# Softmax sums of one group of heads: from products with ones to adds on VectorE

## The chip, the cores and the metric

The kernel runs on one core of a Trainium2 chip. A core has a matrix engine (TensorE, PE in the profile, with PEld for its weight loads), VectorE (DVE), ScalarE (ACT), GpSimd (POOL) and SyncE (SP), which here only issues transfers. The metric is the device time of one execution in microseconds. The kernel before the change takes 2181.35 us (median of three runs, 2180.84 to 2181.51).

## The reference

One decoder layer on x of shape (4, 1024, 512) in float32, with a context of shape (4, 1024, 384): a gated self-attention, a cross-attention to the context, and a small feed-forward network, each behind a layer norm and each added to its input. The change lies in the cross-attention, for the last of the four batches:

```python
attn = jnp.einsum('bhqd,bhkd->bhqk', q, k) * scale      # 16 heads of 32
attn = jax.nn.softmax(attn, axis=-1)
x = jnp.einsum('bhqk,bhkd->bqhd', attn, v).reshape(B, Nq, Cq)
return x @ Wo + bo
```

The feed-forward network after it is

```python
s = jnp.einsum('btd,dm->btm', x, Win) + bin_
h = jax.nn.relu(s[..., None] * W1 + b1)                  # 16 hidden rows
g = jnp.einsum('btmh,mh->btm', h, W2) + b2
out = jnp.einsum('btm,md->btd', g, Wout) + bout
```

## The kernel before, in words

There are eight units: self-attention (phase 0) for the four batches, then cross-attention (phase 1) for the four batches. A unit is worked in two halves of 512 queries, a half in four groups of four heads (`g` is 0 to 3), a group in eight steps (`kt`), one for each block of 128 keys. A step (`step`, L725) does this:

- `scores` (L606): TensorE multiplies keys and queries for the four heads, two heads to a tile (L614). ScalarE takes the exponentials of each pair into a tile `e` of 128 x 1024 (L620). The softmax needs, for each query, the sum of the exponentials over all keys, and this sum is made in one of two ways. Either VectorE adds the tiles of the steps into an accumulator `es` (L626 in step 1, L628 after it), and at the end one product with a column of ones sums over the 128 partitions (L672). Or TensorE multiplies every exponential tile with a column of ones and accumulates the result in the PSUM tile `sm` (L650).
- `times` (L639) for the step before: TensorE multiplies values and exponentials into `av` (L642), and every second step it makes the products with ones (L650) for the second pair of heads, for two blocks of keys, four products at a time in four column groups of the array.
- then a share of other work, spread over the steps by `run` (L976): the projections, norms and network of the half before and of the next unit.

Which way is taken is set by `shared`. In phase 0, and in the last unit (`u` is 7), it is true: the first pair of heads is added on VectorE, the second pair is summed by products with ones. In the units 4 to 6 it is false and VectorE adds both pairs. The very last group of the kernel (`closing`) always adds both pairs.

One step after a group's last `times`, `normalize` (L656) copies `av` and, if `shared`, `sm` out of PSUM on ScalarE (L659, L661). One step later `add_up` (L669) makes the products with ones of the accumulators, copies them out (L673), and sends the sums to DRAM and back so that they lie spread over the partitions: with `shared` two writes (L678, L683) and two reads (L684, L688), without it one write (L678) and one read (L680). Three steps later `divide` (L693) takes the reciprocals and sends them out (L712) and back, broadcast (L716, four transfers). Three steps after that `multiply` (L721) scales `av` into `q` (L722).

Every engine and every queue works in the order in which the program issues instructions; the order is written by hand. The transfers named here are all issued by SP.

Beside group 1 of each half of the last unit lies the work of the half of the queries before: the output projection (`project`: L101 on TensorE, then the residual on VectorE, L813, and the statistics, L817 and L818), the hidden rows of the network (`hidden`: ScalarE L905, VectorE L909 and L911) and the network's outputs (`outputs`, L918: TensorE L922, VectorE L928, transfer out L930). After them come the normalized rows (`norm`, VectorE L310), their trip to DRAM and back (`away` L314, `back` L319), which with a transpose of blocks on VectorE (L325) turns them, and the first product of the network (`inputs`, L884).

The projections, the network's outputs and some of the scores use the two PSUM banks called `f`, which alternate:

```python
        def bank():
            since[0] = 0
            return pf.tile([P, HALF], F32, tag="f", name="f")
        def score_banks():
            if spare[0] and not open_[0] and since[0] >= 2:
                two = [bank(), bank()]
```

`score_banks` borrows both for one pair of heads where no other work of that step needs them; otherwise the scores use one of two tiles `s`.

Of the kernel before, what the change touches and what calls it, by code (L numbers as in the profile page):

```python
# [63 lines left out]
def moderate_path(tc: tile.TileContext, a: dict, out: bass.AP, flag: bass.AP):  # L64
    nc = tc.nc
    x = a["x"]
    with ExitStack() as st:
# [20 lines left out]
# [4 lines that stand above are left out]
                return two, [(slice(i, i + 1), b) for i, b in enumerate(two)]  # L92
            since[0] += 1
            s = ps.tile([P, 2, HALF], F32, tag="s", name="s")
            return [s[:, i, :] for i in range(2)], [(slice(0, 2), s)]
# [250 lines left out]
        order = [(ph, b) for ph in range(2) for b in range(B)]  # L346
# [5 lines left out]
        def after(steps, f, behind=False):  # L352

            soon.append((tick[0] + steps, behind, f))
# [236 lines left out]
        def attention(u, hf):  # L591

            ph, b = order[u]
# [1 line left out]
            steps = []  # L595
            sums = 2 if ph == 0 else 1

            shared = ph == 0 or u + 1 == len(order)

            def apart(g):  # L600
                return 2 if u + 1 < len(order) else 3

            def closing(g):
                return (u, hf, g) == (len(order) - 1, 1, HG - 1)

            def scores(g, kt):  # L606
                q, k = me["q", hf], me["k"]
                es = []
                for i in range(2):
                    two, reads = score_banks()  # L610
                    for j in range(2):
                        r = slice((2 * i + j) * DH, (2 * i + j + 1) * DH)
                        for m in range(0, P, 64):
                            nc.tensor.matmul(  # L614
                                two[j][m : m + 64], lhsT=k[r, g, kt * P + m : kt * P + m + 64], rhs=q[r, g, :],
                                start=True, stop=True,
                            )
                    e = p4.tile([P, 2, HALF], F32, tag="e", name="e", bufs=6)
                    for h, s in reads:
                        nc.scalar.activation(e[:, h, :] if len(reads) == 1 else e[:, h.start, :], s, AF.Exp, scale=SCALE)  # L620
                    es.append(e)
                me["e", kt] = es
                for i in range(1 if shared and not closing(g) else 2):
                    if kt == 1:
                        me.setdefault("es", {})[i] = p1.tile([P, 2, HALF], F32, tag=f"es{i}", name="es")
                        nc.vector.tensor_tensor(me["es"][i], me["e", 0][i], es[i], ALU.add)  # L626
                    elif kt > 1:
                        nc.vector.tensor_tensor(me["es"][i], me["es"][i], es[i], ALU.add)  # L628
                if ph == 0 and kt > 0:
                    if kt == 1:  # L630
                        me["eg"] = p1.tile([P, 2, HALF], F32, tag="es1", name="eg")
                    for h in range(2):
                        eg, gate = me["eg"][:, h, :], lambda t: me["sw"][:, t, HG * g + h, 1:2]
                        if kt == 1:
                            nc.scalar.activation(eg, me["e", 0][0][:, h, :], AF.Identity, scale=gate(0))  # L635
                        nc.vector.scalar_tensor_tensor(eg, es[0][:, h, :], gate(kt), eg, ALU.mult, ALU.add)  # L636
                return es

            def times(g, kt, es):  # L639
                for h in range(HG):  # L640
                    r = slice(h * DH, (h + 1) * DH)
                    nc.tensor.matmul(  # L642
                        av[r, :], lhsT=me["v"][:, kt, HG * g + h, :], rhs=es[h // 2][:, h % 2, :],
                        start=(kt == 0), stop=(kt == NT - 1),
                    )
                if shared and kt % 2 and not closing(g):

                    for j in range(4):
                        t, h = kt - 1 + j // 2, j % 2
                        nc.tensor.matmul(  # L650
                            sm[j * DH : j * DH + sums, :],
                            lhsT=me["sw"][:, t, HG * g + 2 + h, :] if ph == 0 else ones, rhs=me["e", t][1][:, h, :],
                            start=(kt == 1), stop=(kt == NT - 1),
                        )

            def normalize(g):  # L656
                i = (u * 2 + hf) * HG + g
                both = p1.tile([P, 3, HALF], F32, tag="both", name="both")
                nc.scalar.copy(both[:, 0, :], av)  # L659
                if shared:  # L660
                    nc.scalar.copy(both[:, 1, :], sm)  # L661
                    added = [me["es"][0][:, 0, :], me["es"][0][:, 1, :]]
                    if ph == 0:
                        added += [me["eg"][:, 0, :], me["eg"][:, 1, :]]
                else:
                    added = [me["es"][h // 2][:, h % 2, :] for h in range(HG)]
                after(1, lambda: add_up(g, i, both, added), behind=True)

            def add_up(g, i, both, added):  # L669

                for j, e in enumerate(added):
                    nc.tensor.matmul(sm[j * DH : j * DH + 1, :], lhsT=ones, rhs=e, start=True, stop=True)  # L672
                nc.scalar.copy(both[:, 2, :], sm)  # L673

                c, s1, s2 = cs_[i % 2], sum1_d[i % 4], sum2_d[i % 4]
                rows = both.rearrange("(j r) s q -> j r s q", r=DH)
                n = len(added)
                nc.sync.dma_start(s1[0:n], rows[0:n, 0, 2, :])  # L678
                if not shared:
                    nc.sync.dma_start(c[:, 0, 0, :], s1[0:n].rearrange("h (q e) -> (h q) e", e=INNER))  # L680
                else:
                    for k in range(sums):
                        nc.sync.dma_start(s2[k], rows[:, k, 1, :])  # L683
                    nc.sync.dma_start(  # L684
                        c[0:64, 0:sums, 0, :], s1[0:n].rearrange("(s h) (q e) -> (h q) s e", h=2, e=INNER)
                    )
                    for k in range(sums):
                        nc.sync.dma_start(  # L688
                            c[64:, k, :, :], s2[k].rearrange("(p h) (q e) -> (h q) p e", h=2, e=INNER)
                        )  # L690
                after(apart(g), lambda: divide(g, i, both, c))

            def divide(g, i, both, c):  # L693
                if shared:
                    both_ = p2.tile([P, sums, INNER], F32, tag="c2", name="both_")
                    nc.vector.tensor_tensor(both_, c[:, 0:sums, 0, :], c[:, 0:sums, 1, :], ALU.add)
                else:
                    both_ = c[:, 0:1, 0, :]
                if ph == 0:

                    den = p2.tile([P, INNER], F32, tag="den", name="den")
                    nc.vector.scalar_tensor_tensor(
                        den, both_[:, 0, :], 1e-8, me["iap", hf][:, g, :], ALU.mult, ALU.mult
                    )
                    nc.vector.tensor_tensor(den, den, both_[:, 1, :], ALU.add)
                else:
                    den = both_[:, 0, :]
                rec = p2.tile([P, INNER], F32, tag="rec", name="rec")
                nc.vector.reciprocal(rec, den)
                nc.vector.tensor_reduce(marks[:, i : i + 1], den, AX.X, ALU.add)  # L710
                nc.vector.tensor_reduce(marks[:, NS + i : NS + i + 1], rec, AX.X, ALU.add)
                nc.sync.dma_start(rec_d[i % 4].rearrange("j (q e) -> (j q) e", e=INNER), rec)  # L712

                all_ = p1.tile([P, HALF], F32, tag="recb", name="recb")
                for j in range(HG):
                    nc.sync.dma_start(  # L716
                        all_[j * DH : (j + 1) * DH, :], rec_d[i % 4][j : j + 1, :].to_broadcast([DH, HALF])
                    )
                after(apart(g), lambda: multiply(g, both, all_), behind=u + 1 < len(order))

            def multiply(g, both, all_):  # L721
                nc.vector.tensor_tensor(me["q", hf][:, g, :], both[:, 0, :], all_, ALU.mult)  # L722
                me["divided", hf] = g
# [1056 lines left out]
```

## Time and profile before

| | us |
|---|---|
| median of three runs | 2181.35 |
| the profiled execution, own time | 2181.99 |
| its span, first to last instruction | 2180.1 |
| TensorE busy | 2158.6 (99%) |
| VectorE busy | 1483.6 (68%) |
| ScalarE busy | 1278.9 (59%) |
| GpSimd busy | 121.9 (6%) |

The times in rows of the profile count from the start of the span. A row of the timeline names start, length, engine, line of the kernel, operation, output and input tiles, and in brackets the engine's idle time before it with what ended that. Rows of TensorE count records; a float32 product leaves two, so a set of four products shows as x8. The last unit's first half has its scores from about 1922 us on, its second half runs to about 2130 us. Group 1, which the change touches, has its eight steps from about 1948 to 1980 us in the first half and from about 2052 to 2084 us in the second. The clock granted to TensorE is full (1.00) in both stretches.

### The profile page before, as it was taken

To read this page: it belongs to the slowest core of one execution; us is meant where nothing else is said; L and a number is where in the kernel's file an instruction comes from. 1 tells how busy PE (TensorE), PEld (TensorE's weight loads), DVE (VectorE), ACT (ScalarE), POOL (GpSimd) and SP (SyncE) were. 2 spreads that over 40 slices of the span, in tenths; PEclk is the share of its full clock that TensorE was granted. 3 is DMA by queue.
4 is the path that set the end of the run, shared out by engine and by line. 5 is a ranking of instruction groups with operands and counts; after the bars stand their busy time and mean duration, and the time that the engine had idled before them with its cause. 6 is when DMAs were issued, how large, how long until landed. Compare 5 with 4: busy or idle time off the path is not lost.

```text
span 2180.1 us, 52850 instructions
## 1 busy us (share of the span) xinstructions
PE 2158.6 (99%) x22750; PEld 557.8 (26%) x22750; DVE 1483.6 (68%) x2158; ACT 1278.9 (59%) x1583; POOL 121.9 (6%) x175
## 2 busy tenths in 40 slices
PE   9999999999999999999999999999999999999997
PEld 4322222222222222222222222222222222222223
DVE  3477575786756866556666666877877777766567
ACT  0156545655456554566666666675757667577774
POOL 2000010040210101000000000000000000000000
PEclk9999999999999999999999999999999999999999
DMA  6412133031330221121222132222223141312231
GB/s 168 122 47 71 48 99 114 19 89 66 98 112 21 86 71 42 60 66 46 71 80 94 41 93 66 69 65 79 70 84 108 50 104 36 84 51 70 71 89 46
DMA packets 154137, 161.71 MB, mean 74 GB/s; under 512 B 47003, under 2 KB 92699, under 8 KB 152741
## 3 DMA queue, kind: packets, MB, share of 16 engines
q1 hardware_dynamic: 149828, 156.14, 24.8%
q8 instruction: 180, 2.95, 0.6%
q0 software_dynamic: 2080, 0.98, 0.3%
q10 hardware_dynamic: 1984, 1.12, 0.2%
q14 instruction: 65, 0.52, 0.1%
HBM read 115.40 MB, written 42.74 MB: 73 GB/s over the span
## 4 chain that ended last, share of the span: by engine, by line
PE 94%; DVE 2%; DMA 1%; ACT 1%; issue 1%; SPq 0%; POOL 0%; ACTq 0%; DVEq 0%
PE f L101 36%; PE s L614 24%; PE av L642 22%; PE sm L650 6%; PE sm L672 3%; PE s L101 1%; ACT e L620 1%; PE f L922 1%; PE f L884 1%; DVE es L628 1%; DVE g L911 1%; DMA rec_d<-rec 0%; DMA w<-in_attn_Wo 0%; PE f L614 0%; PE f L489 0%
## 5 line engine op out<-in xcount | busy, mean ns | idle before, releaser
L620 ACT ACTIVATE e<-s 128x1024 f32<-128x1024 f32 x998 | 970.3, 1023 | 662.3 <-PE s L614 460.8
L628 DVE TENSOR_TENSOR es<-es,e 128x1024 f32<-128x1024 f32 x534 | 642.7, 1227 | 278.5 <-ACT e L620 277.3
L614 PE MATMUL s<-q,k 32*64 32x512 f32 x7984 | 594.9, 613 | 1.1 <-ACT e L620 0.5
L642 PE MATMUL av<-e,v 128*32 128x512 f32 x4096 | 550.8, 603 | 0.6 <-ACT e L620 0.6
L101 PE MATMUL f<-xT,w 128*32 128x512 f32 x2816 | 333.7, 592 | 0.0
L636 DVE SCALAR_TENSOR_TENSOR eg<-e,sw,eg 128x512 f32<-128x512 f32 x448 | 315.5, 745 | 9.3 <-ACT eg L635 9.3
L626 DVE TENSOR_TENSOR es<-e 128x1024 f32<-128x1024 f32 x89 | 106.8, 1223 | 242.4 <-ACT e L620 215.8
L101 PE MATMUL f<-w,q 128*32 128x512 f32 x1984 | 240.3, 593 | 0.0
L614 PEld LDWEIGHTS s<-q,k 32*64 32x64 f32 x7984 | 129.4, 130 | 422.8 <-ACT e L620 211.9
L642 PEld LDWEIGHTS av<-e,v 128*32 128x32 f32 x4096 | 88.1, 108 | 404.7 <-issue 400.8
L101 PEld LDWEIGHTS f<-xT,w 128*32 128x32 f32 x2816 | 92.3, 110 | 210.3 <-issue 207.0
L650 PE MATMUL sm<-e,sw 128*2 128x512 f32 x1024 | 133.3, 592 | 0.0
L101 PE MATMUL f<-w,xT 128*32 128x512 f32 x896 | 106.0, 592 | 0.6 <-DVE q L299 0.6
L101 PEld LDWEIGHTS f<-w,q 128*32 128x32 f32 x1984 | 66.0, 110 | 148.5 <-issue 141.5
L905 ACT ACTIVATE hid<-sT,units 128x256 f32<-128x256 f32 x128 | 76.9, 608 | 27.9 <-DVE g L911 24.3
L101 PE MATMUL f<-w,ctxT 128*32 128x512 f32 x768 | 92.7, 592 | 0.0
L101 PE MATMUL f<-ctxT,w 128*32 128x512 f32 x768 | 92.3, 592 | 0.0
L821 POOL TENSOR_TENSOR r<-res,bo_bc 128x512 f32<-128x512 f32 x32 | 41.1, 1284 | 759.6 <-DVE res L813 723.4
L911 DVE SCALAR_TENSOR_TENSOR g<-hid,units,g 128x256 f32<-128x256 f32 x120 | 57.5, 479 | 14.0 <-ACT hid L905 8.7
L672 PE MATMUL sm<-es,fixed 128*1 128x512 f32 x348 | 65.0, 591 | 0.2
L305 POOL TENSOR_SCALAR rs<-fmv 128x4 f32<-128x4 f32 (+1 forms) x17 | 7.9, 468 | 870.4 <-DVE fmv L818 870.4
L813 DVE TENSOR_TENSOR res<-f,res 128x512 f32<-128x512 f32 x62 | 42.5, 685 | 18.3 <-PE f L101 14.2
(263 smaller groups left out, 1145.6 us busy)
## 6 DMA issues: line engine op xcount, KB each, us to landing
recb<-rec_d SPq DMA_DIRECT2D x252, 64.0 KB
xT<-rows_d SPq DMA_DIRECT2D x60, 256.0 KB
rows_d<-r SPq DMA_DIRECT2D x60, 256.0 KB
w<-in_xattn_Wo SPq DMA_DIRECT2D x9, 1024.0 KB
w<-wout_d SPq DMA_DIRECT2D x8, 1024.0 KB
res<-in_x SPq DMA_DIRECT2D x32, 256.0 KB
x1b_d<-r SPq DMA_DIRECT2D x32, 256.0 KB
res<-x1b_d SPq DMA_DIRECT2D x32, 256.0 KB
```

Source lines behind the costliest of these rows:

```text
L101: nc.tensor.matmul(to[r], lhsT=lhsT[:, j, :] if len(lhsT.shape) == 3 else lhsT[:, r], rhs=rhs, **flags)
L614: nc.tensor.matmul(two[j][m : m + 64], lhsT=k[r, g, kt * P + m : kt * P + m + 64], rhs=q[r, g, :], start=True, stop=True,)
L620: nc.scalar.activation(e[:, h, :] if len(reads) == 1 else e[:, h.start, :], s, AF.Exp, scale=SCALE)
L626: nc.vector.tensor_tensor(me["es"][i], me["e", 0][i], es[i], ALU.add)
L628: nc.vector.tensor_tensor(me["es"][i], me["es"][i], es[i], ALU.add)
L636: nc.vector.scalar_tensor_tensor(eg, es[0][:, h, :], gate(kt), eg, ALU.mult, ALU.add)
L642: nc.tensor.matmul(av[r, :], lhsT=me["v"][:, kt, HG * g + h, :], rhs=es[h // 2][:, h % 2, :], start=(kt == 0), stop=(kt == NT - 1),)
L650: nc.tensor.matmul(sm[j * DH : j * DH + sums, :], lhsT=me["sw"][:, t, HG * g + 2 + h, :] if ph == 0 else ones, rhs=me["e", t][1][:, h, :], ...
L672: nc.tensor.matmul(sm[j * DH : j * DH + 1, :], lhsT=ones, rhs=e, start=True, stop=True)
L813: nc.vector.tensor_tensor(r, res["po"], r, ALU.add)
L905: nc.scalar.activation(hid, res["s"], AF.Relu, bias=units[:, 1, h : h + 1], scale=units[:, 0, h : h + 1])
L911: nc.vector.scalar_tensor_tensor(res["g"], res["hid"], units[:, 2, h - 1 : h], res["g"], ALU.mult, ALU.add)
```

## The change

`shared` becomes a function of the group. In the last unit it is false for group 1, in both halves, and unchanged for the groups 0, 2 and 3 and for the other units. In group 1 VectorE therefore adds both pairs of heads, `times` makes no products with ones, `normalize` does not copy `sm`, `add_up` makes four products in place of two and one write and one read in place of two and two, and `divide` has no addition of two parts.

```diff
-            shared = ph == 0 or u + 1 == len(order)
+            def shared(g):
+                return ph == 0 or (u + 1 == len(order) and not (g == 1))
...
-                for i in range(1 if shared and not closing(g) else 2):
+                for i in range(1 if shared(g) and not closing(g) else 2):
...
-                if shared and kt % 2 and not closing(g):
+                if shared(g) and kt % 2 and not closing(g):
...
-                if shared:
+                if shared(g):
                     nc.scalar.copy(both[:, 1, :], sm)
...
-                if not shared:
+                if not shared(g):
                     nc.sync.dma_start(c[:, 0, 0, :], s1[0:n].rearrange("h (q e) -> (h q) e", e=INNER))
...
             def divide(g, i, both, c):
-                if shared:
+                if shared(g):
```

## The prediction

> **What bounds the kernel now.** I read four views in this order: the page's chain that ended last, busy time over the two places that change, the order of work on TensorE and VectorE inside them, and the chain of waits just behind them.
>
> The chain, by engine, and the row of the work that is added:
>
> ```profile
> PE 94%; DVE 2%; DMA 1%; ACT 1%; issue 1%; SPq 0%; POOL 0%; ACTq 0%; DVEq 0%
> L628 DVE TENSOR_TENSOR es<-es,e 128x1024 f32<-128x1024 f32 x534 | 642.7, 1227 | 278.5 <-ACT e L620 277.3
> ```
>
> TensorE sets 94% of the end, so work taken from it should shorten the kernel, unless the place itself is bound otherwise. One add of a pair of heads lasts 1.23 us; where two follow each other (1898.48) the pair lasts 2.36, and the next instruction behind a single one starts 1.14 after it (1958.72, then 1959.86). I price an add at 1.14.
>
> Busy time from group 1's second scores to group 2's second scores, first half and second half (columns: stretch, length, then PE, PEld, DVE, ACT, POOL busy, clock, DMA):
>
> ```profile
> 1951.93:1983.22 31.29, 31.29 (x320) 7.50 (x316) 20.60 (x34) 18.79 (x23) 1.55 (x3) 1.00 0.11 36
> 2056.34:2087.64 31.30, 31.30 (x321) 7.49 (x317) 18.49 (x29) 16.34 (x18) 1.55 (x3) 1.00 0.13 42
> ```
>
> TensorE is full in both. VectorE has 10.7 and 12.8 us free: room for seven adds of 1.14 (8.0), but not much. The question is whether the free time lies before or behind the moment at which TensorE needs VectorE. The two orders (start, length, engine, line), first half:
>
> ```profile
> 1975.18 1.04 PE L650 MATMUL sm<-e,fixed 128*1 128x512 f32 x8
> 1976.15 1.13 PE L922 MATMUL f<-wout,g 64*128 64x512 f32 x4
> ...
> 1982.25 1.04 PE L650 MATMUL sm<-e,fixed 128*1 128x512 f32 x8
> 1983.22 0.66 PE L614 MATMUL f<-q,k 32*64 32x512 f32 x4
> ```
> ```profile
> 1975.46 1.24 DVE L628 TENSOR_TENSOR es<-es,e 128x1024 f32<-128x1024 f32 x1 [0.43 <-ACT e L620]
> 1977.31 1.29 DVE L928 TENSOR_TENSOR res<-f,res 128x512 f32<-128x512 f32 x2 [0.61 <-PE f L922]
> 1978.51 0.68 DVE L722 TENSOR_TENSOR q<-both,recb 128x512 f32<-128x512 f32 x1
> 1979.42 1.23 DVE L628 TENSOR_TENSOR es<-es,e 128x1024 f32<-128x1024 f32 x1 [0.23 <-ACT e L620]
> 1980.56 1.28 DVE L928 TENSOR_TENSOR res<-f,res 128x512 f32<-128x512 f32 x2
> ```
>
> The feed-forward output (L922, at 1976.15 and 1979.25) fills both `f` banks each time; VectorE's pair L928 empties them. L922's second turn needs the first L928 pair (done 1978.6), and the scores at 1983.22, which borrow both `f` banks, need the second (done 1981.84, 1.4 us before). An add placed in front of L928 on VectorE therefore goes straight into TensorE's path once that 1.4 is used. The second half is the same 104.4 us later: L928 ends at 2086.25, the scores are at 2087.64.
>
> The chain of waits behind group 1, first half, and its counterpart's first link in the second:
>
> ```profile
> 1986.91 0.54 SPq L678
> 1987.50 2.51 DMA sum_d<-both
> 1990.02 0.63 SPq L688
> 1990.74 0.54 SPq L314
> 1991.37 2.23 DMA rows_d<-r
> ...
> 1995.77 4.71 DMA rec_d<-rec
> 2001.78 2.05 DMA recb<-rec_d
> ...
> 2089.12 4.44 DMA rows_d<-r
> ```
>
> Here TensorE is not the bound: group 1's sums, the normalized rows (L314, L319) and the reciprocals go through one SP queue in order; the last return holds L722 (1.75 us idle), then a transpose, then the feed-forward product L884, where TensorE stands 0.58 us (before 2006.45). In the second half the chain comes from the last L928: outputs leave (L930), four loads follow (L788), then L314; its write holds VectorE's norm L310 until 2093.0, and L884 ends in 0.76 us of waiting (x32 lasts 2.67 against 1.91 at 1917.85).
>
> **The change part by part.**
>
> Removed on TensorE: per half four sets of four products with ones (L650; 8 records a set). A set costs the distance to the next start: 0.86 (1958.43 to 1959.29), 0.85 (1966.81), and 0.97 at 1975.18 and 1982.25, where the L642 before it then hands on 0.1 later without it (1978.25 to 1979.25 is 1.00, against 0.89 in front of L650). So 4 x 0.86 = 3.44 a half, 6.9 in all, if nothing else stops TensorE.
>
> Added on TensorE: the closing sum has four products in place of two. They run beside each other in four column groups: with four, scores at 1925.49 to next scores at 1928.53 took 3.04; with two, 1983.22 to 1986.23 took 3.01. Nothing. ScalarE loses the copy L661 (0.62) in each half; idle time of 0.5 to 2 us stands beside it. VectorE loses L696 in group 1's division (0.2). Nothing is credited for either.
>
> Added waits: the second accumulator es1 was last read in unit 6 (1897.4) or the half before, so its first write finds it free. Behind a late add on VectorE stand, in order, L813 (residual, frees a projection bank that nobody needs for four steps), L911 (the network sum, which lets ScalarE's next hidden row start; in the first half six of these, in the second two), L928, L722 and L310. POOL's root (L305) waits for the last L818, which moves by 0.03 (1975.05 for 1975.02). The exponentials have six tiles, three steps' worth; VectorE falls at most one step behind, so ScalarE finds them free.
>
> VectorE, first half, placed by hand with steps shortened by 0.86 where a set is gone. Second exponentials are ready 0.9 after the first. From the first add (1954.14): its partner to 1956.4, L813 to L911 to 1958.6, adds of step 2 to 1961.0, two L911 to 1962.0; step 3 can begin at 1963.1 (a hidden row waits for L911 and holds the exponentials 0.7), adds to 1965.4, L813 group to 1967.3, division to 1967.9, step 4 and L911 to 1970.6, step 5 with L911 and the L813 group to 1975.05. From there VectorE has no gap: adds to 1977.33, L928 to 1978.53, L722 to 1979.15, adds to 1981.44, L928 to 1982.64, its two banks free at 1982.1 and 1982.75. As a check: VectorE's idle time from 1954.14 to 1981.84 is 8.0, the added work is 8.0, so the end can hardly move forward. TensorE without sums would reach the second L922 at 1976.8 and stands until 1978.0 to 1978.6; it would reach the borrowed-bank scores at 1981.7 and stands until 1982.75. They end near 1983.9 in place of 1984.4. Of 3.44, 0.5 is left. (All idle filled, 1981.84, gives 1.3; 0.7 of idle unfilled gives nothing: ends 1.3 and -0.2.)
>
> Second half: 9.8 of idle up to L928's end. The same placing gives step 5 ending at 2078.24, first L928 2080.52 to 2081.8, second 2084.63 to 2085.9, against 2086.25. TensorE loses about 0.2 at the second L922 and 1.3 at the borrowed banks; the scores end about 1.7 early.
>
> The SP queue, group 1 of each half: two DMAs (L678, and the read back) in place of four. First half: L678 0.7 to 0.5 earlier; the write of the rows (second L314) stood behind L688, which is gone, and then follows the read at 1988.3 in place of 1990.74. L319, rec_d and the last return move by about the same 2.2, more than TensorE's 0.5 + 0.58: L884 no longer waits. First half: 0.5 + 0.58 = 1.1.
>
> Second half: L930 and L788 stand ahead of L314 and start from L928, 0.35 earlier; the write takes 4.44, so L310 starts 0.35 earlier, and VectorE stands longer before it (3.4 in place of 1.81). The second L314 was held by L688 until 2094.83; now the rows hold it until 2093.9. From there L319 (3 us later, 1.9 long), rec_d (4.7) and the return (2.0) follow: L884 comes 0.95 earlier, and TensorE's 1.7 is spent there. Second half: 0.95; ends 0 (L928 as late as before) and 3.4 + 0.76 = 4.2 (no hold at all).
>
> Sum: 1.1 + 0.95 = 2.1 us. The profiled execution took 2181.99 (span 2180.1 and 1.9 around it), 0.64 above the median of 2181.35; 2179.9 on its scale, 2179.2 on the median's.
>
> [...]
>
> **The rivals.** *TensorE keeps the whole.* For it: 94% of the chain and 31.3 of 31.3 busy, and 10.7 free on VectorE; against it: L928 stands behind the adds. If VectorE waits overlap so that the banks are free in time, 3.44 + 0.58 in the first half and between 0.95 and 4.2 in the second: 2173.1 to 2176.4, say 2175. [...]
>
> *Slower: VectorE cannot use its idle time.* Before an add VectorE idles for an exponential that TensorE paces. If TensorE, held at the banks, paces it as before, only part of the 8.0 is filled. L928's end then moves out by the unfilled part; beyond 1.4 (first half) TensorE is later than before, in the second half the row chain from L928 on by the same amount at once less the 1.8 of spare idle. With half filled: 4.0 - 1.4 = 2.6 and 8.0 - 4.9 = 3.1, together 5.7: 2187. It decides against the change once more than about 1.9 of 8.0 is unfilled in each half. Against it: the scores before the first L922 need no bank, so the gaps in steps 1 to 5 are open.
>
> *No effect:* TensorE's gain is all spent at L884 and the queue is no faster: 2180.5 to 2181.4. It lies in the forecast's own range.
>
> **How the numbers follow.** The forecast, with ends from both halves (first half 0.4 to 1.9, second 0 to 4.2, counted up to 4.3: 2177.0 to 2181.4), 0.63; whole gain kept 0.25; slower 0.12. A measurement of this kernel can tell about 0.2% (4.4 us) from no change: below 2177.0 lies the second case and a little of the first (0.26), above 2185.7 most of the third (0.11), the rest 0.63. The range takes in the nearer half of the gain case and the near end of the slower one: 2175.0 to 2182.5.
>
> **What would show it.** Right: L928's second pair ends between 1981.8 and 1983 although TensorE has 3.4 less to do; TensorE waits appear at L922 and at the `f` scores named after L928; no gap on VectorE from 1975 on; L314's second pair right after two sum DMAs; no wait at the first half's L884, 1.5 us or so at the second's. Wrong: no wait after L928 (then near 2175), or L928 ending after 1984 (slower).

## The result, and the profile after

The changed kernel takes 2177.51 us (median of 22 runs, 2176.21 to 2182.19), the kernel before 2181.47 (22 runs beside them, 2180.07 to 2182.87). The medians differ by 4.0 us. The ratio is put at 0.9985, with a 95% interval of 0.9978 to 0.9991: 3.3 us less, between 2.0 and 4.8. The forecast was 2179.2 in a range of 2175.0 to 2182.5.

The profiled execution took 2177.92 us (span 2176.1, against 2180.1). Of those 4.0 us of span not all belong to the change. An ACT copy that every group of heads has (`both<-av`, L659) shows where the two traces part: from the first group of the first unit (132.21 before, 131.12 after) up to group 0 of the last unit it is 1.07 to 1.10 us earlier. That much came in the first 40 us, where nothing was changed: the products at its beginning (L1086) lasted 5.16 before and 4.29 after, at a granted clock of 1.00 in both. The twelve traces of the experiments have this copy 0.5 to 1.3 us earlier than the trace before, too, and none of their kernels changes anything there. So I measure each half of the last unit by itself, from the copy of group 0's `av` to the copy `sT` behind the feed-forward product (L884 before, L885 after; all lines behind L598 moved down by one):

| | first half | second half |
|---|---|---|
| before | 1950.30 to 2008.42: 58.12 | 2054.71 to 2112.40: 57.69 |
| after | 1949.22 to 2005.21: 55.99 | 2051.49 to 2107.55: 56.06 |
| gain | 2.13 | 1.63 |

Together 3.8. What follows gains nothing more; the tail is 0.8 us longer, half of that in the last network outputs, which kept TensorE busy for 3.13 us at a granted clock of 0.62 before, and for 3.52 us at 0.55 after.

From the page after: the row of the adds (12 more L629, two more L627; the duration is the same).

```profile
L629 DVE TENSOR_TENSOR es<-es,e 128x1024 f32<-128x1024 f32 x546 | 656.4, 1227 | 268.9 <-ACT e L621 267.7
```

Busy time from group 1's second scores to group 2's second scores (columns as before the change: stretch, length, PE, PEld, DVE, ACT, POOL busy):

```profile
1950.86:1980.74 29.88, 28.94 (x289) 7.20 (x285) 26.52 (x39) 18.29 (x23) 3.11 (x3) 1.00 0.09 29
2053.12:2082.06 28.94, 28.60 (x289) 6.93 (x285) 24.50 (x34) 15.82 (x18) 3.11 (x3) 1.00 0.09 30
```

The first was 31.29, the second 31.30. VectorE now works 26.5 of 29.9 us, and TensorE is no longer full. TensorE, first half:

```profile
1972.50 1.50 PE L923 MATMUL f<-wout,g 64*128 64x512 f32 x4
...
1976.67 1.72 PE L923 MATMUL f<-wout,g 64*128 64x512 f32 x4 [0.63 <-DVE res L929]
...
1980.74 1.24 PE L615 MATMUL f<-q,k 32*64 32x512 f32 x6 [0.31 <-DVE res L929]
...
1982.37 1.04 PE L673 MATMUL sm<-es,fixed 128*1 128x512 f32 x8
```

and VectorE beside it:

```profile
1972.14 0.68 DVE L814 TENSOR_TENSOR res<-f,res 128x512 f32<-128x512 f32 x1
...
1973.69 2.33 DVE L629 TENSOR_TENSOR es<-es,e 128x1024 f32<-128x1024 f32 x2
1975.93 1.28 DVE L929 TENSOR_TENSOR res<-f,res 128x512 f32<-128x512 f32 x2
1977.13 0.68 DVE L723 TENSOR_TENSOR q<-both,recb 128x512 f32<-128x512 f32 x1
1977.73 2.35 DVE L629 TENSOR_TENSOR es<-es,e 128x1024 f32<-128x1024 f32 x2
1980.00 1.28 DVE L929 TENSOR_TENSOR res<-f,res 128x512 f32<-128x512 f32 x2
```

No row of VectorE has idle time in front of it here. Both waits of TensorE (0.63, 0.31, and more inside the row that stretches from 1.13 to 1.72) end on L929, which empties the `f` banks. The first L923, too, stretches from 1.13 to 1.50, and that is not L929: its second product starts at 1972.9, just behind the residual L814 (done at 1972.8), which empties the other `f` bank. What the shorter products saved is given back at this place.

SP's queue behind group 1, first half and then the second, up to the return of the reciprocals:

```profile
1984.47 0.54 SPq L679 DMA_DIRECT2D sum_d<-both  x1
1986.23 0.31 SPq L681 DMA_DIRECT2D cs<-sum_d  x1
1986.63 0.86 SPq L314 DMA_DIRECT2D rows_d<-r  x2
1989.42 1.92 SPq L319 DMA_DIRECT2D xn<-rows_d  x4
...
2083.01 1.90 SPq L789 DMA_DIRECT2D res<-x1b_d  x4
2085.01 0.85 SPq L314 DMA_DIRECT2D rows_d<-r  x2
2085.96 0.54 SPq L679 DMA_DIRECT2D sum_d<-both  x1
2089.78 0.31 SPq L681 DMA_DIRECT2D cs<-sum_d  x1
2090.18 0.86 SPq L314 DMA_DIRECT2D rows_d<-r  x2
2092.97 2.13 SPq L319 DMA_DIRECT2D xn<-rows_d  x4
2095.14 0.54 SPq L713 DMA_DIRECT2D rec_d<-rec  x1
2099.70 1.71 SPq L717 DMA_DIRECT2D recb<-rec_d  x4
```

In the first half the rows' second write (L314 at 1986.63) follows the one read at once. In the second the chain still sets L885: VectorE stands 3.45 us for the rows and 1.58 for the reciprocals, and TensorE stands inside L885.

```profile
2089.50 1.20 DVE L310 TENSOR_SCALAR r<-res,fmv,rs 128x512 f32<-128x512 f32 x2 [3.45 <-DMA rows_d<-r]
2103.07 0.69 DVE L723 TENSOR_TENSOR q<-both,recb 128x512 f32<-128x512 f32 x1 [1.58 <-DMA recb<-rec_d]
```
```profile
2003.24 1.91 PE L885 MATMUL f<-xn,win 128*32 128x256 f32 x32
...
2105.58 1.92 PE L885 MATMUL f<-xn,win 128*32 128x256 f32 x28 [0.42 <-DVE xn L325]
```

### The profile page after: what moved, and what is told of

It reads as the page before. It is cut to its first block, busy times and chain, and to the rows that moved or that the text cites. A ratio compares the mean times of both kernels' runs of the same rounds, so it can differ in the third digit from the quotient of the medians.

```text
span 2176.1 us, 52749 instructions
## 1 busy us (share of the span) xinstructions
PE 2152.5 (99%) x22694; PEld 554.6 (25%) x22694; DVE 1498.8 (69%) x2170; ACT 1277.9 (59%) x1581; POOL 124.7 (6%) x175
## 3 DMA queue, kind: packets, MB, share of 16 engines
q8 instruction: 180, 2.95, 0.5%
## 5 line engine op out<-in xcount | busy, mean ns | idle before, releaser
L629 DVE TENSOR_TENSOR es<-es,e 128x1024 f32<-128x1024 f32 x546 | 656.4, 1227 | 268.9 <-ACT e L621 267.7
L627 DVE TENSOR_TENSOR es<-e 128x1024 f32<-128x1024 f32 x91 | 109.0, 1223 | 242.8 <-ACT e L621 216.2
L673 PE MATMUL sm<-es,fixed 128*1 128x512 f32 x356 | 65.0, 591 | 0.0
L814 DVE TENSOR_TENSOR res<-f,res 128x512 f32<-128x512 f32 x62 | 42.5, 685 | 14.0 <-PE f L101 10.6
```

The source lines that it names most:

```text
L814: nc.vector.tensor_tensor(r, res["po"], r, ALU.add)
```

## The experiments

My theory after the result: two things take TensorE's shorter work back. VectorE's adds stand in front of L929, so the `f` banks come free late; and in the second half SP's queue, from L929 over the rows to the reciprocals, sets L885. The rivals: the gain is simply TensorE's and something small is lost anywhere; or the transfers alone matter. All kernels were timed beside the kernel before, whose medians lay between 2181.61 and 2181.84.

**One half at a time.**

```diff
-                return ph == 0 or (u + 1 == len(order) and not (g == 1))
+                return ph == 0 or (u + 1 == len(order) and not (g == 1 and hf == 0))
```

This is the kernel with the first half alone; the other has `hf == 1` in its place.

> Only the first half's group 1 is changed. Theory (VectorE's adds stand in front of L929 and hold TensorE at the f banks; what is left of the 3.44 us, and the wait at the feed-forward product L885, is gained in each half by itself): the scores behind the first half's L885 come 2.1 us earlier against the start of group 1, nothing changes in the second half, the time is 2.1 us below before. Rival (the gain comes from the second half's row transfers alone, since the first half's adds fill VectorE): 0 to 0.5 us here.

> Only the second half's group 1 is changed. Theory: the scores behind the second half's L885 come 1.6 us earlier against the start of its group 1, the time is 1.6 us below before; with the first half's 2.1 it adds up to what both do (3.8). Rival (the halves are not independent, for the first half's gain needs the second's later waits): the two do not add up.

Measured: 2179.65 (ratio 0.9991, 0.9982 to 1.0000) and 2180.44 (0.9995, 0.9986 to 1.0004). By the halves' lengths the changed first half took 55.99, exactly as in the change, so the halves are independent there. The changed second half took 56.97, 0.7 less than before and 0.9 more than in the change; the rows' second write (L314) took 3.63 to land there, 2.79 in the change. But the halves that were not changed also moved: 58.22 in the first of these kernels (57.69 before) and 58.43 in the second (58.12). Single executions differ by this much (0.5 and 0.3) where L885 waits for the rows that transfers return: its idle column shows 0.68 and 0.88 in these two halves. The two gains add up to 3.1 by the ratios (2.0 and 1.1), where the change has 3.3, and to 3.2 by the medians (2.0 and 1.2), where it has 4.0: the intervals are too wide to tell these apart, and the second gain is too small to be told from nothing by itself.

**The adds without the shorter products, and the shorter products without the adds.**

```diff
-                for i in range(1 if shared and not closing(g) else 2):
+                for i in range(1 if shared and not closing(g) and not (u + 1 == len(order) and g == 1) else 2):
```

> As before, with the products with ones kept, but VectorE makes the seven added adds in each half as well, and nobody reads them. Theory: in the first half the last L928 ends 1.2 us later, just before the borrowed banks are needed, which costs nothing; in the second half it ends 1.3 us later and the row transfers start from it: 1.3 us above before. Rival (VectorE has 10.7 and 12.8 us free and hides the adds): no change. Second rival (VectorE cannot fill its gaps, since they wait for exponentials): 4 to 6 us above before.

Measured: 2183.47, ratio 1.0010 (1.0001 to 1.0019): 1.8 above before by the medians. By the trace the first half took 58.01 (58.12 before), the second 58.99 (57.69), that is +1.3, where halves without a change had moved by 0.3 to 0.5. VectorE before the borrowed banks of the second half:

```profile
2083.11 2.35 DVE L628 TENSOR_TENSOR es<-es,e 128x1024 f32<-128x1024 f32 x2
2085.38 1.28 DVE L928 TENSOR_TENSOR res<-f,res 128x512 f32<-128x512 f32 x2
```

L928 ends at 2086.66; this half began 0.88 earlier than before (2053.83 for 2054.71), so that is 1.3 later than before. VectorE did fill its gaps (the 8.0 us of adds moved the end by 1.3), and the adds are not free: the row chain starts from L928.

```diff
-                    elif kt > 1:
+                    elif kt > 1 and not (i == 1 and ph == 1 and not shared(g) and u + 1 == len(order) and not closing(g)):
```

> As the change, but VectorE makes only the first of the seven added adds in each half; the other six are left out, so the sums of two heads in group 1 are incomplete. Theory (the adds in front of L929 take TensorE's gain): TensorE no longer waits at L923 and at the borrowed f banks, keeps 3.4 us a half, the row transfers follow, and the waits at L885 go too: 8 us below before, 4 below the change. Rival (the gain is limited by the transfers and not by VectorE): as the change, 3 to 4 us below before. Second rival (TensorE's own products cost less than their distances): 4 to 5 us.

Measured: 2175.63 (0.9976, 0.9967 to 0.9985), 6.0 below before, not 8. Seven of its 11 runs took 2174.5 to 2175.8, four 2177.9 to 2180.1; the profiled execution, 2177.91, is one of the four. In it the first half took 53.61: 4.5 below before, as expected. The second took 58.79, more than before, though TensorE was 2.5 us early at the end of group 1:

```profile
2100.60 0.60 PE L885 MATMUL f<-xn,win 128*32 128x256 f32 x4
2105.12 2.65 PE L885 MATMUL f<-xn,win 128*32 128x256 f32 x28 [3.92 <-DVE xn L325]
```

So VectorE's adds are what holds the first half, and in the second there is the other holder, behind which all that TensorE won was spent in this execution. The expectation took that chain as following TensorE; it does not.

**Adds one step later.** The second pair's add of a step is issued at the start of the next step, and so behind the L929 of the step that it belongs to:

```diff
+                    if i == 1 and u + 1 == len(order) and g == 1:
+                        held_adds.append(lambda first=me["e", 0][1]: add(1, kt, first))
...
                     issue_due(False)
+                    while held_adds:
+                        held_adds.pop(0)()
                     es = scores(g, kt)
```

> As the change, but in group 1 of the last unit the second pair's add of each step is issued one step later on VectorE, so that one add fewer stands in front of each L929. Theory: each L929 ends 1.1 us earlier, TensorE waits 1.1 less at the f banks in each half, the row transfers start 1.1 earlier: 2 us below the change, 6 below before. Rival (another wait, for exponentials or transfers, sets TensorE there): as the change.

Measured: 2176.01 (0.9974, 0.9965 to 0.9983), 1.5 below the change. First half 54.85 (1.14 less, the length of one add), second 55.74 (0.3 less). In the first half one add in front of L929 is one add on TensorE's path. In the second TensorE came to group 2 0.6 earlier than in the change (group 1 lasted 30.54 against 31.13) and lost part of it at L885 (0.62 in its idle column, 0.42 in the change).

**The transfers.** With the second write and read of the sums kept in group 1, their data unused:

```diff
                 nc.sync.dma_start(s1[0:n], rows[0:n, 0, 2, :])
+                more = u + 1 == len(order) and g == 1
+                if more:
+                    nc.sync.dma_start(s2[0], rows[:, 0, 2, :])
...
+                    if more:
+                        nc.sync.dma_start(
+                            c[64:, 1, :, :], s2[0].rearrange("(p h) (q e) -> (h q) p e", h=2, e=INNER)
+                        )
```

> As the change, but group 1 of the last unit still sends a second write and a second read of its sums (the data are not used), as before the change. Theory (part of the gain is that the rows' second write, L314, stands behind two transfers fewer in SP's queue): in the first half L314's second pair comes 1.5 us later than with the change and TensorE waits 0.5 us at L885 again; in the second half it comes 0.7 later, and so does L885: 1.2 us above the change, 2.6 below before. Rival (the transfers are hidden; TensorE's shorter work is all of the gain): as the change.

Measured: 2182.22 (0.9999, 0.9990 to 1.0008): the whole gain is gone, with a wide spread (2178.72 to 2183.82). By the trace the first half lost 1.13 against the change (57.12), and TensorE waits at the feed-forward product again (0.55 in its idle column); the second lost 4.0 (60.07). There the rows' second write landed 4.7 us after its issue, in place of 2.8:

```profile
2091.57 0.64 SPq L686 DMA_DIRECT2D cs<-sum_d  x1
2092.78 0.97 SPq L314 DMA_DIRECT2D rows_d<-r  x2
2097.50 1.93 SPq L319 DMA_DIRECT2D xn<-rows_d  x4
```

The direction was right, the size not. Two ways of freeing the queue followed. First the loads L789 (the last half's residual rows, wanted only in the tail) behind the rows' read:

```diff
-                out += (ending[0]["load"] if hf else []) + weave(last["ln"], pause(5)) + last["xT"]
+                out += weave(last["ln"], pause(5)) + last["xT"] + (ending[0]["load"] if hf else [])
```

> As the change, but in the second half the four loads L789 are issued behind the rows' transfers L314 and L319 in SP's queue instead of ahead of them. Theory (the row chain from L929 over SP's queue holds the second half's L885): the first L314 comes 1.9 us earlier, VectorE's wait at L310 shrinks from 3.4 us, TensorE's wait of 1.0 us at L885 goes: 1 us below the change. Rival (the chain is hidden): no change. Against it: the loads come later and the tail's residual adds might wait for them.

> As the change, with the second pair's adds one step later and the loads L789 behind the rows' transfers. Theory: both gains add up, 3 us below the change, 7 below before. Rival: one of them makes the other idle (the row chain no longer sets L885, so the loads' place is worth nothing): 2 us below the change.

Measured: 2179.56 (0.9988, 0.9979 to 0.9997) and 2178.50 (0.9981, 0.9972 to 0.9991). Both miss: 2.1 and 1.0 above the change. The second halves took 57.79 and 58.23, 1.7 and 2.2 more than in the change. SP's queue of the first of them shows why:

```profile
2090.78 1.92 SPq L319 DMA_DIRECT2D xn<-rows_d  x4
2092.74 3.08 SPq L789 DMA_DIRECT2D res<-x1b_d  x4
2095.92 0.38 SPq L713 DMA_DIRECT2D rec_d<-rec  x1
2101.38 1.72 SPq L717 DMA_DIRECT2D recb<-rec_d  x4
```

The rows were read 2.2 us earlier than in the change, but the loads now stood in front of the reciprocals' write L713 (their values were there at 2092.87), and counted from the half's start that came 0.7 later; its landing took 5.5 us. L723 stood 3.87 us for the return. The link that ends last is L713 to L717, not the rows' own.

So the loads went behind L885:

```diff
-                out += weave(last["tr"], pause(3)) + last["s"] + weave(some(last, 8), pause(14))
+                out += weave(last["tr"], pause(3)) + last["s"] + (ending[0]["load"] if hf else [])
+                out += weave(some(last, 8), pause(14))
```

> As the change, but the four loads L789 are issued only behind the second half's L885, so that neither the rows' transfers nor the write and return of group 1's reciprocals (L713, L717) stand behind them in SP's queue. In the run with the loads only behind L319, the rows came 2.7 us earlier, but L713 stood behind the loads and came later, and L723 with it. Theory (SP's queue up to L717 holds the second half's L885): L713 follows L319 at once, 2 us earlier than with the change; TensorE's 1.0 us at L885 goes; 1 us below the change. Rival (the return of the reciprocals is slow by itself, or the loads come too late for the tail): as the change or above it.

Measured: 2176.19 (0.9974, 0.9963 to 0.9984), 1.3 below the change. The second half took 55.04, 1.0 less than in the change. SP's queue, and L885 without a wait:

```profile
2086.41 0.53 SPq L679 DMA_DIRECT2D sum_d<-both  x1
2088.13 0.31 SPq L681 DMA_DIRECT2D cs<-sum_d  x1
...
2091.34 1.92 SPq L319 DMA_DIRECT2D xn<-rows_d  x4
2093.31 0.87 SPq L713 DMA_DIRECT2D rec_d<-rec  x1
2098.68 1.71 SPq L717 DMA_DIRECT2D recb<-rec_d  x4
2100.43 1.86 SPq L789 DMA_DIRECT2D res<-x1b_d  x4
```
```profile
2105.18 1.91 PE L885 MATMUL f<-xn,win 128*32 128x256 f32 x32
```

The loads also delayed the sums. L681 reads back what L679 wrote, and it is issued 1.72 us after L679 here, 3.82 after it in the change (2085.96, then 2089.78), where L679 stood just behind the loads.

The eight runs lie within 1.2 us (2175.57 to 2176.75); the change's 22 spread over 6.0.

> As the run with the four transfers kept, which came 4.7 us above the change in place of 1.2, with the loads L789 behind L885. In that run's profiled execution the second half lost 4.0 us against the change: 1.2 in SP's queue ahead of L314, and 1.9 more because L314's second write took 4.7 to land in place of 2.8. Theory (the long landing comes from the loads' traffic ahead of it): without the loads the landing is 2.8 again, the two transfers cost 1.1 us in the first half and 0.3 to 0.7 in the second: 1.4 to 1.8 above the run with the loads last alone, near 2177.8. Rival (two reads of the sums make the landing long by themselves): 4 us or more above that run, near 2180.

Measured: 2177.58 (0.9981, 0.9972 to 0.9990), 1.4 above the run with the loads last alone; halves 56.59 and 55.56, that is 0.6 and 0.5 more. The rows' second write landed in 2.95. The two transfers cost about a microsecond in the queue; the other three that they cost with the loads in place go with the loads. (The first half is the same code in both kernels with four transfers, and lost 1.13 in the one trace and 0.6 in the other: a single trace is good to about half a microsecond here.) Long landings of that write (3.6 to 4.7) were seen in four profiled executions, all with the loads ahead of it, but four others with the loads ahead had 2.7 to 3.0. What tips one execution over stays open.

**Both holders away.**

> As the run without six of the seven added adds (sums of two heads in group 1 of the last unit incomplete), with the loads L789 behind L885. That run gained 4.5 us in the first half and, in its profiled execution, nothing in the second, where L885 stood for the return of the reciprocals. Theory (VectorE's adds and SP's queue are the only two things that take TensorE's gain): both halves now gain 4.1 to 4.5: 8 to 8.6 us below before. Rival (a third thing holds the second half): 6 us, as without moving the loads.

> As the run with the second pair's adds one step later (1.5 us below the change), with the loads L789 behind L885. Theory: there TensorE still waits 1.2 us at the second half's L885; without that 2.6 us below the change, 6.6 below before. Rival: the row chain is as late as with the loads in place: 1.5 below the change.

Without the adds: 2172.42 (0.9957, 0.9944 to 0.9971); halves 53.60 and 54.05, that is 4.5 and 3.6 below before, 8.2 in all (9.4 by the ratio, 6.3 to 12.2). In the first half TensorE runs through the place without a wait; in the second one wait is left, at L885, which lasts 0.52 longer than undisturbed:

```profile
1972.97 1.13 PE L923 MATMUL f<-wout,g 64*128 64x512 f32 x4
...
1976.14 1.13 PE L923 MATMUL f<-wout,g 64*128 64x512 f32 x4
...
1979.24 0.66 PE L615 MATMUL f<-q,k 32*64 32x512 f32 x4
...
2101.13 2.43 PE L885 MATMUL f<-xn,win 128*32 128x256 f32 x32
```

This is close to what the products' removal is worth where neither VectorE nor the queue takes it. VectorE still stood 1.44 us for the return of the reciprocals in the second half, so the last 0.52 are the queue's too, and no room is left for a third holder of any size.

With the adds made, one step late, and the loads last: 2174.41 (0.9965, 0.9951 to 0.9979); halves 54.85 and 54.54. That is 7.6 us below before by the ratio (4.6 to 10.7), 6.4 by the halves, and 3.1 below the change by the medians: the fastest kernel here that computes everything.

## Why the prediction was right, point by point

The direction and the mechanism held; the time lay inside the range, 1.7 below the forecast. The size did not hold as well: 2.1 us less was forecast, 3.3 came by the ratio and 4.0 by the medians, and all three terms of the sum (0.5, 0.58 and 0.95) were too small. The range also took in the time of no change (2181.4), so the hit alone says little; it is the waits on L929 and the edits above that support the mechanism.

*TensorE's saving, 3.44 a half.* Right. Without six of the seven adds and with the loads last, the halves are 4.52 and 3.64 shorter than before. Of that, by the distance of starts, the wait at the feed-forward product gives 1.19 in the first half (1.19 before, none left) and 0.24 in the second (0.76 before, 0.52 left). The rest is 3.33 and 3.40.

*VectorE's order, first half.* I placed the second L928 pair to end at 1982.64. It ended at 1981.28, which is 1982.37 with the 1.09 us of the earlier start put back. In the second half I had 2085.9, and the trace gives 2082.60, or 2085.8 with 3.22 put back. The claim that the end can hardly move, since idle time and added work are both 8.0, was right, and the run with unused adds shows the same from the other side. The second L922 was placed at 1978.0 and started at 1977.76; the borrowed scores at 1982.1, and they started at 1981.83 (both with the 1.09 put back).

*What is left at the scores, 0.5 and 1.7.* Mis-sized in the first half. The closing sum (L673) comes 0.96 earlier (1982.37 with 1.09 put back, against 1984.42), not 0.5. I let all four heads wait for the second bank (1982.75); the scores of the first bank ran while the second was still held, and the closing sum came 1.6 after the first of them. In the second half it was 1.9 where I had 1.7. One wait of the first half I had put at nothing: I wrote of the bank that the residual L813 empties that nobody needs it for four steps, but L922 takes it in the next step and stood 0.37 for it. By the distances of starts, against the run without the adds and with the loads last, TensorE waits in the change 0.37 for L814 and 2.1 for L929 in the first half, and 1.5 for L929 in the second: 3.44 less these is 0.97 and 1.94.

*The wait at L884, first half, 0.58.* Mis-sized, and a reading error: I took the idle time that the row of TensorE prints. From the first records of L884 (2005.27) to the next scores (2008.30) are 3.03 us, against 1.84 where it runs undisturbed (after: 2003.24 to 2005.08). The wait cost 1.19, of which the idle column of that row shows 0.58. The weight-load row in front of it had said 1.06. That the wait would go, because the rows' write follows the sums at once, was right: predicted at 1988.3, it went out at 1987.7 with the shift put back.

*The second half, 0.95.* Mis-sized: 1.63. L314's first write came 0.42 earlier for 0.35 and L310's second 0.28 for 0.35, as worked out; the second write came 1.43 earlier for 0.95, since the first of its two transfers leaves when the first of the two rows is ready (at about 2090.1 in the trace after), and I had let it wait for both. The queue would not have let it go sooner either: the read L681, held until 2089.78 by the late sums, ended at 2090.09. From there L319, L713 and L717 moved by 1.5 to 1.7 and L885 with them. L885's wait there grew to 1.0, not the 1.5 I named.

*The whole.* 1.1 + 0.95 = 2.1 was forecast, 2.13 + 1.63 = 3.8 came in the trace, 3.3 in the ratio. The rival in which TensorE keeps the whole (2175) was refuted by the waits on L929 (2.1 and 1.5 us): the engine that was relieved waited for the one that was loaded. But its size is what the two edits of the last experiments bring back. The slower rival (VectorE cannot fill its gaps) did not happen: the gaps in steps 1 to 5 of the first half were filled but for 1.2 us. The likeliest case, a change within 0.2%, is the one that came: 0.15% by the ratio, and its interval, 0.09% to 0.22%, does not reach zero.

*The price of an add.* A pair of adds moved the following instruction by 2.28 (1957.64 to 1959.92), so 1.14 each, as priced; the pairs lasted 2.33 to 2.36, a single add 1.23. Where instructions follow each other on VectorE the distance of starts decided here, not the duration of one.

## What to carry to other kernels

Here the work that moved from a full engine to one with free time was paid at the instructions of the second engine for which the first one waited (0.37 us for L814 and 2.1 for L929 in the first half, 1.5 for L929 in the second); count the added work in front of such an instruction, not over the stretch. Behind it, follow the queue of transfers to the last link before the next common point: here four loads that nobody needed yet stood ahead of small transfers in SP's queue and took 1.0 us of what the second half had won (56.06 with them there, 55.04 with them last). Read a wait on TensorE from the distance of starts against an undisturbed case: here its idle column showed 0.58 of 1.19.

## What the runs showed of the hardware that was not expected

A small write issued behind bulk transfers in the same queue landed late. L713's 8 KB took 4.5 to 5.9 us (from its issue to the issue of L717, which waits for it) in the second half of all fourteen traces, behind the four reads L319 or, in two of them, behind the loads L789; in the first half it took 4.7 before, 5.1 after and 5.8 with four transfers, behind L319 too. In the other groups of the last unit, where the queue had issued nothing for 3.4 us or more, it took 1.4 to 2.4 in the traces before and after (2037.06 to 2038.52 in the trace after). That the reads cause it is likely but not shown, since no run moved them.

For the loads and the sums it is shown by moving them. In the second half the sums' write L679 was followed by its read after 1.8 to 5.1 us in the eight traces with the loads ahead of it (1.8 and 2.2 where it was issued 2.8 us behind the loads, 3.4 to 5.1 where that was 1.0 to 1.5), and after 1.7 us in all six with the loads behind.

The loads ahead of the rows' write may also widen the spread of the times: the change's 22 runs spread over 6.0 us, and the four kernels with the loads last over 1.0 to 2.1 (five to eleven runs each). But the kernel before, whose loads stand ahead as well, spread over 1.8 to 3.3 in its five sets of runs, so this is not shown.
